# A transformer's second attention on one core: scores from halved operands in 32 rows, and normalisation on two engines

## The chip, the cores and the metric

The kernel runs on one core of a Trainium2 chip. A core has a matrix engine (TensorE, PE in the profile, with its weight loads shown as PEld), a vector engine (VectorE, DVE), an engine for activation functions (ScalarE, ACT), a general engine (GpSimd, POOL) and one that mainly issues transfers (SyncE, SP). Each works through its own queue of instructions in a fixed order; semaphores tie them together. Matrix products land in PSUM, everything else lives in SBUF, and DRAM is reached by DMA. The metric is the device time of one execution in microseconds (us), lower is better.

## The reference

The input x is 16 sequences of 256 tokens with 128 features, in float32. Four residual steps follow one another:

```
x = x + attention_a(layernorm(x))      # 2 heads of 64, rotary embedding on half of each head
x = x + ffn(layernorm(x))              # 128 -> 512 -> 512 -> 512 -> 128, ternary weights
x = x + attention_b(layernorm(x))      # 16 heads of 8, masked
x = x + ffn(layernorm(x))
```

The second attention is the one that the change touches:

```
mask = arange(n)[:, None] <= arange(n)[None, :]
scores = einsum('bhki,bhqi->bhkq', k, q) / sqrt(8)
scores = where(mask, scores, -10000)
probs = softmax(scores, axis=2)                 # over the third axis, inside 'bhkq'
combined = einsum('bhkq,bhkl->bhql', probs, v)
```

The softmax runs over the keys as scores are laid out here, and masked scores count as -10000 and not as minus infinity. The kernel therefore needs the maximum of each row of scores, and a correction for the masked ones.

## The kernel before

**Blocks.** The 4096 tokens are cut into 8 blocks of 512 (two sequences each). Each block goes through attention a, FFN f, attention b and FFN g. Blocks are independent, so the stages of several blocks overlap.

**The plan.** The kernel doesn't issue instructions as it goes. A class `Plan` (from line 95) records every operation with the engine, an assumed duration, and the tiles that it reads and writes. `laid` (line 166) then lays them out one after the other: among the operations that are ready it takes, for each engine, those that could start within 0.144 us of the earliest (a change of activation table or of PE's tiling mode weighted by `WEIGH`), and among these the one of the lowest rank by `ORDER` (line 337). Operations recorded with `either` (line 147) name two or three engines, and the layout takes the one that has room. `emit` (line 275) issues everything in that order; therefore nearly every instruction carries line 287 in the profile, and one tells groups by their tiles.

**Buffers.** SBUF tiles come from groups with a fixed number of slots: `w6`, `w4` and `w8` all appear as `w` in the profile, as do the four single PSUM banks. `s` is the one four-bank PSUM tile for scores of both attentions. `h` holds the FFN's hidden layers in two fp32r parts, a rounded one and the remainder, `u` an FFN layer before it is split, `hl` its last layer.

**Layernorm** (`layernorm_T`, line 651). Per block DVE computes mean and variance (`st`, `mv`), POOL the inverse root (`rstd`), DVE normalises in four instructions of 128x128 (`xh`), PE transposes, and an eviction writes `xT`. The attentions use `xhattn`, the FFNs `xhffn`.

**Attention b, inputs** (`attention_b_inputs`, line 802). PE makes q and k for all 16 heads, 8 features each, so that head 4g + a sits in rows 32g + 8(3 - a) and following. q is evicted twice (`qb`), scaled by `qscale`; k four times (`kb`), each time with all heads but one set to zero by `kmask`. A product over 32 rows with the masked k gives the scores of one head of a group g, and four groups g run in the four 32-row parts of the array.

**Attention b, maxima** (`attention_b_max`, line 833). For each sequence and each a of four, eight fp32 matmuls in 32 rows (per head one of 128 and one of 256 columns) write scores to `s`, four bf16 matmuls add a mask (`eye`, `hide`), and DVE takes the maxima of three 128-key blocks (`m3`). The negative maxima go into unused rows of a transposed tile (`nm`), and two DVE operations (`q2`) add them to q, so that one row of the next product subtracts them.

**Attention b, probabilities** (`attention_b`, line 892). For each a, eight fp32 matmuls in 32 rows write the transposed scores minus the maxima, ACT takes exp (1536 columns), POOL clears the masked half of the diagonal blocks (affine select), and PE multiplies with `vp` (v with a column of ones, in 32-column mode). The rest divides, transposes and projects.

**FFN** (`ffn`, line 1038). fp32r matmuls of 512 columns, two parts per operand, silu and gelu on ACT, products and splits on DVE, ACT or POOL. The ranks place FFN work as filling between the attentions' steps.

**The fork.** `product` (line 1001) has a general form for weights that fp32r can't hold exactly; a branch at run time picks it. With the given weights it isn't taken.

Of the kernel before, what the change touches and what calls it, by code (L numbers as in the profile page):

```python
# [94 lines left out]
class Plan:  # L95
# [4 lines left out]
    SWITCH = 0.15  # L100
    WEIGH = 0.78
# [45 lines left out]
    def either(self, *ways):  # L147

        (engine, us, name, a, k), *rest = ways
        r = self(engine, us)  # L150
        getattr(r, name)(*a, **k)
        for engine, us, name, a, k in rest:
            other = Op(engine, us, r.op.rank)
            other.calls.append((name, a, k))
            r.op.others.append(other)
# [10 lines left out]
    def laid(self):  # L166
# [28 lines left out]
        for _ in range(len(self.ops)):  # L195
            best = None
            for e, ops in ready.items():
# [23 lines left out]
                if not cands:  # L221
                    continue

                first = min(a + self.WEIGH * c for a, c, _ in cands)
                at, cost, op = min(
                    (x for x in cands if x[0] + self.WEIGH * x[1] <= first + 0.144),
# [63 lines left out]
class _Recorder:  # L290
# [19 lines left out]
P = 128  # L310
B, T, E = 16, 256, 128
TB = 4
# [25 lines left out]
    (INPUT, "a"): (47, 0.9),  # L338
    (MAIN, "a"): (52, 1.0),
    (NORM, "f"): (298, 0),  # L340
    (FILL, "f"): (118, 3.3),
    (INPUT, "b"): (76, 0.9),
    (MAXIMA, "b"): (-22, 0),
    (MAIN, "b"): (14, 17.0),
    (NORM, "g"): (81, 0),
    (FILL, "g"): (180, 9.1),
}
LATER_AT = -89
# [23 lines left out]
def hybrid_kernel(ctx: ExitStack, tc: tile.TileContext, x, rows, cols, wa, wb, w12, h1, h2, w3, out):  # L372
# [5 lines left out]

    p = Plan(nc)

    def group(tag, slots, in_turn=False):
        g = Group(slots, in_turn)
        g.tag = tag
        return g
# [8 lines left out]
    g_24, g_16, g_32 = group("w6", 4), group("w4", 3), group("w8", 3)  # L393
    q_qkv, q_pT, q_qkT, q_qb, q_pa, q_kb = Group(2), Group(3), Group(2), Group(2), Group(2), Group(2)
    g_rope, g_oT, g_small = group("rope", 6), group("oT", 2), group("small", 16)
    g_vb, g_q2, g_wv, g_o, g_oTb = (group(n, k) for n, k in (("vb", 2), ("q2", 2), ("wv", 2), ("o", 2), ("oTb", 1)))
# [166 lines left out]

    pi = fixed([P, 4], "pi", I32)
    p("POOL", 0.1).iota(pi[:], pattern=[[0, 4]], base=0, channel_multiplier=1)
    wanta = fixed([P, 4], "wanta", I32)
    p("POOL", 0.1).iota(wanta[:], pattern=[[1, 4]], base=0, channel_multiplier=0)
    wantr = fixed([P, 4], "wantr", I32)
    p("POOL", 0.1).iota(wantr[:], pattern=[[-3, 4]], base=31, channel_multiplier=0)
    ai = fixed([P, 4], "ai", I32)  # L570
    ri = fixed([P, 4], "ri", I32)
    kmask = fixed([P, 4], "kmask")
    mrow4 = fixed([P, 4], "mrow4")
    kbias = fixed([P, 4], "kbias")
    qscale = fixed([P, 2], "qscale")
    qbias = fixed([P, 2], "qbias")
    mrow = fixed([P, 2], "mrow")
    s8 = 1.0 / math.sqrt(DB)
    o = p("DVE", 1.25)
    o.tensor_scalar(ai[:], pi[:], 3, 3, ALU.arith_shift_right, ALU.bitwise_and)  # L580
    o.tensor_scalar(ri[:], pi[:], 31, None, ALU.bitwise_and)
    o.tensor_tensor(kmask[:], ai[:], wanta[:], ALU.is_equal)
    o.tensor_tensor(mrow4[:], ri[:], wantr[:], ALU.is_equal)
    o.scalar_tensor_tensor(kbias[:], kmask[:], cols_sb[:, C_BK : C_BK + 1], mrow4[:], ALU.mult, ALU.add)
    o.tensor_scalar(qscale[:, 0:1], kmask[:, 3:4], -s8, s8, ALU.mult, ALU.add)
    o.tensor_scalar(qscale[:, 1:2], kmask[:, 3:4], s8, None, ALU.mult)
    o.tensor_scalar(qbias[:], qscale[:], cols_sb[:, C_BQ : C_BQ + 1], None, ALU.mult)
    o.tensor_reduce(mrow[:, 0:1], mrow4[:, 0:3], AX.X, ALU.max)
    o.tensor_copy(mrow[:, 1:2], mrow4[:, 3:4])
# [61 lines left out]
    def layernorm_T(i, what, bias=None):  # L651
# [16 lines left out]
        xh = sb([P, TB, E], f"xh_{what}{i}", g["xh"])  # L668
        for t in range(TB):
            p("DVE", 0.26).tensor_scalar(  # L670
                xh[:, t, :], XR[i][:, t, :], mv[:, t, 0:1], rstd[:, t : t + 1], ALU.subtract, ALU.mult
            )
# [54 lines left out]
    def attention_a(i, qkv, qkT):  # L727

        sc = p.tile(psum, [P, SEQS, HA, 2, T], F32, f"sa{i}", g_scores)
        for s in range(SEQS):  # L730
            o = p("PE", 0.87, "2r")
# [70 lines left out]
    def attention_b_inputs(i):  # L802

        xT = layernorm_T(i, "b", ob[:])
        q = sb([P, 2, TOK], f"qb{i}", g_16, q_qb)
        pq = bank(f"pqb{i}", ahead)
        p("PE", 0.45, "1", claim=[q]).matmul(pq[:], lhsT=wb_sb[:, 0:128], rhs=xT[:], start=True, stop=True)
        for c in range(2):
            by, plus = qscale[:, c : c + 1], qbias[:, c : c + 1]
            p.either(  # L810
                ("DVE", 0.72, "tensor_scalar", (q[:, c, :], pq[:], by, plus, ALU.mult, ALU.add), {}),
                ("ACT", 0.67, "activation", (q[:, c, :], pq[:], AF.Identity), {"bias": plus, "scale": by}),
            )
        k = sb([P, 4, TOK], f"kb{i}", g_32, q_kb)
        pk = bank(f"pkb{i}", ahead)
        p("PE", 0.45, "1", claim=[k]).matmul(pk[:], lhsT=wb_sb[:, 128:256], rhs=xT[:], start=True, stop=True)
        for a in range(4):
            by, plus = kmask[:, a : a + 1], kbias[:, a : a + 1]
            p.either(
                ("ACT", 0.67, "activation", (k[:, a, :], pk[:], AF.Identity), {"bias": plus, "scale": by}),  # L820
                ("DVE", 0.72, "tensor_scalar", (k[:, a, :], pk[:], by, plus, ALU.mult, ALU.add), {}),
            )
# [8 lines left out]
        return q, k, v  # L831

    def attention_b_max(i, s, q, k, v):
# [10 lines left out]
        for a in range(4):  # L844
            c = a // 3
# [340 lines left out]
```

## Time and profile before

| what | value |
|---|---|
| three timed runs | 823.2 us median, 822.59 to 823.42 |
| profiled execution | 823.35 us, of which the span of its instructions is 821.6 |
| mean granted PE clock in the span | 0.983 of full speed |
| PE busy | 762.0 us (93%), 6212 records |
| DVE busy | 538.2 us (66%) |
| ACT busy | 538.0 us (65%), of which 160.4 us are 125 table loads of 1.283 us |
| POOL busy | 222.9 us (27%) |
| matmuls of transposed scores `s<-q,w` | 1024 records, mean 347 ns |
| matmuls of scores for the maxima `s<-w,w` | 1024 records, mean 348 ns |
| DVE's maxima `m<-s` | 64 of 1755 ns |
| ACT's exp of the second attention `w<-s` | 64 of 1452 ns |
| POOL's causal select | 64 of 1119 ns |
| normalisation on DVE | 64 of 454 ns (`xhattn`), 64 of 389 ns (`xhffn`) |

Busy time of an engine is the union of its records. Matmuls overlap in the pipeline, so a group's cost on PE is best read from its start to the next group's start. An fp32 matmul leaves two records. PE's clock is lower only in the first tens of us. DMA is busy at the start, while inputs load, and with the outputs towards the end.

### The profile page before, as it was taken

Reading aid. Unit: us, or ns where it says so; the run is one execution under the profiler, and the core shown is the slowest. Engines: PE = TensorE matmul, PEld = TensorE weight load, DVE = VectorE, ACT = ScalarE, POOL = GpSimd, SP = SyncE. Lnnn points to the kernel's source line nnn. Section 1 sums busy time; section 2 is a strip of 40 time slices with the busy share of each in tenths; the row PEclk is TensorE's granted clock in tenths of the full one; section 3 lists DMA queues with packets and bytes.
Section 4 is the critical chain, followed back from the end, with each engine's and each line's share of the span. In section 5 each row is a group of like instructions: output and inputs, shape, how many; then the busy total and the mean of one; then the engine's idle time right before and its main releaser. Section 6 shows DMA issues by size and latency. Waiting matters only on the chain.

```text
span 821.6 us, 15080 instructions
## 1 busy us (share of the span) xinstructions
PE 762.0 (93%) x6212; PEld 536.1 (65%) x6212; DVE 538.2 (66%) x1129; ACT 538.0 (65%) x744; POOL 222.9 (27%) x322
## 2 busy tenths in 40 slices
PE   4688999999999999999999998999999999999997
PEld 2355666667577676667675765776776577676775
DVE  7897866877778486637847775763773576262551
ACT  3455887745946746974687475549468546989743
POOL 7654444110411403320233033113113301323200
PEclk9689999999999999999999999999999999999999
DMA  9400000000000000000000000000000000000000
GB/s 286 130 2 1 1 2 0 2 1 1 2 1 1 1 2 1 1 2 1 1 2 2 1 1 2 2 14 2 14 1 14 2 1 14 1 14 1 14 15 18
DMA packets 12191, 11.69 MB, mean 14 GB/s; under 512 B 720, under 2 KB 9424, under 8 KB 12112
## 3 DMA queue, kind: packets, MB, share of 16 engines
q1 hardware_dynamic: 10624, 7.61, 3.0%
q0 software_dynamic: 1200, 2.62, 0.9%
q8 instruction: 51, 0.84, 0.4%
q10 hardware_dynamic: 288, 0.39, 0.3%
q14 instruction: 28, 0.23, 0.1%
HBM read 8.53 MB, written 2.10 MB: 13 GB/s over the span
## 4 chain that ended last, share of the span: by engine, by line
PE 60%; DVE 20%; ACT 14%; issue 2%; POOL 1%; DMA 1%; SPq 0%; POOLq 0%; DVEq 0%; ACTq 0%
PE w L287 45%; PE s L287 15%; ACT w L287 6%; ACT L287 5%; DVE w L287 4%; DVE h L287 2%; DVE small L287 2%; DVE xhattn L287 2%; ACT u L287 2%; DVE u L287 2%; DVE m L287 1%; DMA x<-in_x 1%; ACT h L287 1%; DVE o L287 1%; DVE xlffn L287 1%
## 5 line engine op out<-in xcount | busy, mean ns | idle before, releaser
L287 PE MATMUL w<-h,h_sb 128*128 128x512 f32 x1024 | 281.2, 412 | 3.7 <-DVE h L287 1.3
L287 PEld LDWEIGHTS w<-h,h_sb 128*128 128x128 f32 x1024 | 181.3, 189 | 56.0 <-issue 8.7
L287 ACT ACT_TABLE_LOAD x125 | 160.4, 1283 | 4.1 <-PEq L1177 1.3
L287 POOL TENSOR_SCALAR_AFFINE_SELECT w<-w 128x1024 f32<-128x1024 f32 x64 | 71.6, 1119 | 289.2 <-ACT w L287 282.9
L287 DVE TENSOR_REDUCE m<-s 128x12 f32<-128x1536 f32 x64 | 112.3, 1755 | 50.3 <-PE s L287 49.9
L287 ACT ACTIVATE u<-w,cols_sb 128x512 f32<-128x512 f32 x128 | 87.1, 687 | 76.5 <-PE w L287 75.9
L287 ACT ACTIVATE w<-s 128x1536 f32<-128x1536 f32 x64 | 92.9, 1452 | 32.1 <-PE s L287 30.7
L287 DVE TENSOR_TENSOR h<-u,h 128x512 fp32r<-128x512 f32 x105 | 74.9, 713 | 42.5 <-ACT h L287 39.8
L287 ACT ACTIVATE hl<-w,cols_sb 128x512 f32<-128x512 f32 x64 | 42.1, 687 | 53.7 <-PE w L287 53.4
L287 DVE SCALAR_TENSOR_TENSOR u<-w,cols_sb,u 128x512 f32<-128x512 f32 x64 | 47.7, 746 | 32.9 <-ACT u L287 26.6
L287 PE MATMUL s<-w,w 32*128 32x128 f32 (+1 forms) x1024 | 60.0, 348 | 3.9 <-DVE m L287 2.1
L287 PE MATMUL w<-w_sb,hl 128*128 128x128 f32 x512 | 63.1, 277 | 0.1
L287 PE MATMUL s<-q,w 32*128 32x256 f32 (+1 forms) x1024 | 59.8, 347 | 3.4 <-ACT w L287 2.7
L287 PEld LDWEIGHTS s<-q,w 32*128 32x128 f32 x1024 | 46.2, 184 | 25.5 <-ACT w L287 13.3
L287 PEld LDWEIGHTS w<-w_sb,hl 128*128 128x128 f32 x512 | 60.0, 192 | 2.8 <-ACT hl L287 1.9
L287 PE MATMUL w<-w,vp 128*32 128x256 f32 (+1 forms) x1024 | 55.3, 335 | 4.3 <-POOL w L287 2.8
L287 PE MATMUL w<-xTffn,w_sb 128*128 128x512 f32 x128 | 56.9, 445 | 2.2 <-DVE u L287 1.6
L287 DVE TENSOR_TENSOR x<-w,x 128x512 f32<-128x512 f32 (+1 forms) x40 | 23.2, 579 | 46.5 <-PE w L287 46.0
L287 PE MATMUL w<-xlffn,w_sb 128*128 128x512 f32 x128 | 52.5, 410 | 0.0
L287 PEld LDWEIGHTS s<-w,w 32*128 32x128 f32 x1024 | 34.3, 185 | 24.6 <-DVE m L287 8.9
L287 POOL TENSOR_TENSOR h<-u,h 128x512 fp32r<-128x512 f32 x23 | 29.6, 1290 | 65.3 <-ACT h L287 55.2
L287 PEld LDWEIGHTS w<-w,vp 128*32 128x32 f32 x1024 | 27.1, 110 | 29.5 <-issue 8.7
(153 smaller groups left out, 1068.2 us busy)
## 6 DMA issues: line engine op xcount, KB each, us to landing
w<-in_h SPq DMA_DIRECT2D x2, 1024.0 KB, 14.7
h_sb<-in_h POOLq DMA_DIRECT2D x2, 1024.0 KB, 11.6
out<-x SPq DMA_DIRECT2D x8, 256.0 KB, 2.3
x<-in_x SPq DMA_DIRECT2D x7, 256.0 KB, 8.0
w<-in_w SPq DMA_DIRECT2D x1, 512.0 KB, 8.8
w_sb<-in_w POOLq DMA_DIRECT2D x1, 512.0 KB, 7.2
rows_sb<-in_rows ACTq DMA_DIRECT2D x1, 384.0 KB, 7.1
x<-in_x SPq DMA_DIRECT2D x2, 128.0 KB, 3.2
```

The costliest lines, as they stand in the source:

```text
L287: getattr(getattr(self.nc, self.ENGINES[op.engine]), name)(*a, **k)
```

## The change

The second attention's q and k become two halves each: the value rounded to fp32r (high) and the remainder (low). Each half is written to DRAM twice by SP, by an access pattern that repeats it, and read back by POOL so that a head's 32 rows hold all pairings of high and low: 8 features x 2 x 2. Every head then has its own 32 rows, and one fp32r product over 32 rows gives the exact score. q is scaled by scaling its weights once at the start. The maxima are split into two halves as well and enter the transposed scores through extra matmuls with a selection matrix `pick`. The matmuls' columns change: two of 256 per head for the maxima, and four of 256 per head for the transposed scores (two of k, two of `pick`). The layernorms' normalisation may go to ACT, as scale and shift; POOL makes the shift. The planner's assumed costs, the ranks and the slots of some groups change, and with them the whole order.

```diff
-    SWITCH = 0.15
-    WEIGH = 0.78
+    SWITCH = 0.17
+    WEIGH = {"ACT": 0.81, "PE": 0.07}
...
-                first = min(a + self.WEIGH * c for a, c, _ in cands)
+                weigh = self.WEIGH.get(e, 0.0)
+                first = min(a + weigh * c for a, c, _ in cands)
                 at, cost, op = min(
-                    (x for x in cands if x[0] + self.WEIGH * x[1] <= first + 0.144),
+                    (x for x in cands if x[0] + weigh * x[1] <= first + 0.077),
...
 ORDER = {
-    (INPUT, "a"): (47, 0.9),
-    (MAIN, "a"): (52, 1.0),
...
+    (INPUT, "a"): (-446, 27.2),
+    (MAIN, "a"): (-466, 77.1),
...
-    g_24, g_16, g_32 = group("w6", 4), group("w4", 3), group("w8", 3)
+    g_24, g_16, g_32 = group("w6", 4), group("w4", 3), group("w8", 4)
...
+    pick4 = fixed([P, 4], "pick4")
+    pick = fixed([P, 4, P], "pick", F32R)
...
+    p("DVE", 0.46).tensor_copy(pick[:], pick4[:].unsqueeze(2).to_broadcast([P, 4, P]))
...
+    p("POOL", 0.3).tensor_scalar(wb_sb[:, 0:P], wb_sb[:, 0:P], s8, None, ALU.mult)
...
+        shift = small([P, TB], f"sh_{what}{i}")
+        p("POOL", 0.45).tensor_tensor(shift, mv[:, :, 0], rstd[:], ALU.mult)
+        p("POOL", 0.3).tensor_scalar(shift, shift, -1.0, None, ALU.mult)
         for t in range(TB):
-            p("DVE", 0.26).tensor_scalar(
-                xh[:, t, :], XR[i][:, t, :], mv[:, t, 0:1], rstd[:, t : t + 1], ALU.subtract, ALU.mult
+            by, mean = rstd[:, t : t + 1], mv[:, t, 0:1]
+            p.either(
+                ("DVE", 0.26, "tensor_scalar", (xh[:, t, :], XR[i][:, t, :], mean, by, ALU.subtract, ALU.mult), {}),
+                ("ACT", 0.24, "activation", (xh[:, t, :], XR[i][:, t, :], AF.Identity), {"bias": shift[:, t : t + 1], "scale": by}),
             )
...
-        for c in range(2):
-            by, plus = qscale[:, c : c + 1], qbias[:, c : c + 1]
...
-        for a in range(4):
-            by, plus = kmask[:, a : a + 1], kbias[:, a : a + 1]
...
+        for name, c0, bias in (("q", 0, C_BQ), ("k", P, C_BK)):
...
+            hl = sb([P, 2, TOK], f"{name}hl{i}", g_16, q_hl, F32R)
+            p("PE", 0.45, "1", claim=[hl]).matmul(pp[:], lhsT=wb_sb[:, c0 : c0 + P], rhs=xT[:], start=True, stop=True)
             p.either(
+                ("ACT", 0.67, "activation", (hl[:, 0, :], pp[:], AF.Identity), {"bias": plus}),
+                ("DVE", 0.72, "tensor_scalar", (hl[:, 0, :], pp[:], plus, None, ALU.add), {}),
+            )
+            p("DVE", 0.77).scalar_tensor_tensor(hl[:, 1, :], pp[:], plus, hl[:, 0, :], ALU.add, ALU.subtract)
+
+            shape = [P, 2, 2, TOK]
+            far = p.fixed(dram.tile(shape, F32, name=f"far_{name}{i}"), shape)
+            for part in range(2):
+                p("SP", 0.55, lag=2.4).dma_start(
+                    out=far[:, part] if name == "q" else far[:, :, part],
+                    in_=hl[:, part, :].bitcast(F32).unsqueeze(1).to_broadcast([P, 2, TOK]),
+                )
+            t4 = sb([P, 4, TOK], f"{name}4{i}", g_32, None, F32R)
+            p("POOL", 0.85, lag=6.0).dma_start(out=t4[:], in_=far.rearrange("(g r) x y k -> (r x y) g k", g=4))
...
-            o = p("PE", 1.2, ("4r", "1"))
-            for qt, c0, w in ((0, 0, P), (1, P, T)):
-                for g in range(4):
+            o = p("PE", 0.28 + 0.15 + 0.42, ("4r", "1"))
+            for qt, c0 in ((1, 0), (0, T)):
+                for a in range(4):
+                    rows = slice(32 * a, 32 * a + 32)
                     o.matmul(
-                        lhsT=q[gs, c, t0 + qt * P : t0 + (qt + 1) * P],
-                        rhs=k[gs, a, t0 : t0 + w],
+                        sc[:, a, c0 : c0 + T],
+                        lhsT=q[rows, g, t0 + qt * P : t0 + (qt + 1) * P],
+                        rhs=k[rows, g, t0 : t0 + T],
...
+        o.tensor_copy(both[:, :, :, 0:8:2].bitcast(F32R), m32)
+        o.tensor_tensor(both[:, :, :, 1:8:2].bitcast(F32R), m32, both[:, :, :, 0:8:2], ALU.subtract)
...
-        for c in range(2):
-            p("DVE", 0.39).scalar_tensor_tensor(
-                q2[:, c, :], pm[:, 0:T], mrow[:, c : c + 1], q[:, c, t0 : t0 + T], ALU.mult, ALU.add
-            )
+        evict(mT[:], pm[:, 0:T], T)
...
-                o = p("PE", 0.66, "4r", claim=[pT])
-                for kt, bs, w in ((0, slice(0, 3, 2), T), (1, slice(1, 2), P)):
-                    for g in range(4):
+                o = p("PE", 0.54, "4r", claim=[pT])
+                for kt, c0 in ((1, 0), (0, T)):
+                    for add in range(2):
+                        for a in range(4):
+                            rows = slice(32 * a, 32 * a + 32)
+                            o.matmul(
+                                st[:, a, c0 : c0 + T],
+                                lhsT=pick[rows, g, :] if add else k[rows, g, t0 + kt * P : t0 + (kt + 1) * P],
+                                rhs=mT[rows, :] if add else q[rows, g, t0 : t0 + T],
...
-    nc = bacc.Bacc("TRN2", target_bir_lowering=False, num_devices=1, dynamic_dma_scratch_size=8192)
+    nc = bacc.Bacc("TRN2", target_bir_lowering=False, num_devices=1, dynamic_dma_scratch_size=4096)
```

Left out are the setup of the masks that fall away, the general form's smaller buffers, and the order in which `cols`, `attn_w` and `attn_b` rows are laid on the host (head 4a + g stands in rows 32g + 8a on the way to its own 32 rows).

## The prediction

> **What bounds the kernel now.** I read the shares of busy time first, then the slices, the chain that ended last, one table of windows, and then single groups in the timeline.
>
> From the page: busy time by engine, the TensorE (PE) slices with the clock, and the chain.
>
> ```profile
> PE 762.0 (93%) x6212; PEld 536.1 (65%) x6212; DVE 538.2 (66%) x1129; ACT 538.0 (65%) x744; POOL 222.9 (27%) x322
> ...
> PE   4688999999999999999999998999999999999997
> ...
> PEclk9689999999999999999999999999999999999999
> ...
> PE 60%; DVE 20%; ACT 14%; issue 2%; POOL 1%; DMA 1%; SPq 0%; POOLq 0%; DVEq 0%; ACTq 0%
> PE w L287 45%; PE s L287 15%; ACT w L287 6%; ACT L287 5%; DVE w L287 4%; DVE h L287 2%; DVE small L287 2%; DVE xhattn L287 2%; ACT u L287 2%; DVE u L287 2%; DVE m L287 1%; DMA x<-in_x 1%; ACT h L287 1%; DVE o L287 1%; DVE xlffn L287 1%
> ```
>
> The windows (span, then busy us and instructions of each engine, granted clock, DMA) split the span into the start, the first attention, the second attention's stage and the tail.
>
> ```profile
> 0.00:82.00 82.00, 58.05 (x269) 34.97 (x270) 67.88 (x218) 39.32 (x95) 50.97 (x103) 0.85 0.34 105
> ...
> 164.00:766.00 602.00, 578.25 (x5219) 409.21 (x5218) 381.08 (x703) 404.92 (x461) 135.86 (x154) 1.00 0.01 3
> 766.00:822.00 56.00, 48.01 (x254) 37.88 (x252) 26.60 (x50) 26.75 (x37) 3.63 (x4) 0.99 0.06 17
> ```
>
> PE is busy 96% of the second attention's 602 us (578.25), VectorE (DVE) 63% and ScalarE (ACT) 67%: that stage is PE's, and PE time taken out of it should shorten it. The second attention's scores (tile s) hold 15% of the chain, 126 us. In the timeline, PE alone around one group of scores for the maxima:
>
> ```profile
> 227.75 0.94 PE L287 MATMUL s<-w,w 32*128 32x128 f32 x16
> 228.62 0.61 PE L287 MATMUL s<-hide,eye 128*128 128x256 bf16 x4
> 229.06 0.60 PE L287 MATMUL w<-ident,oT 128*128 128x128 f32 x4
> 229.42 2.58 PE L287 MATMUL w<-h,h_sb 128*128 128x512 f32 x10
> 231.93 0.39 PE L287 MATMUL s<-w,w 32*128 32x128 f32 x3
> ```
>
> and around one transposed group:
>
> ```profile
> 564.68 0.94 PE L287 MATMUL s<-q,w 32*128 32x256 f32 x16
> 565.55 0.74 PE L287 MATMUL w<-h,h_sb 128*128 128x512 f32 x2
> ```
>
> From start to next start a maxima group holds PE 0.87 us, the four mask matmuls (bf16, 256 columns) 0.44, a transposed group 0.87. Four heads run side by side: 16 records of 0.27 to 0.43 us end within 0.94.
>
> **The sum's base.** The profiled execution took 823.35 us (span 821.6 and 1.75 around it), the median of the three timed runs 823.2: the same within 0.02%. I count from 823.35.
>
> **PE: what the halves save.** A mask matmul passes 256 columns in 0.11 us (0.44 / 4). Both old groups stream 256 + 128 columns per head in fp32; at four passes that is 1.5 x 0.11 x 4 = 0.66, so 0.87 - 0.66 = 0.21 goes into entering and leaving the 32-row mode. The new maxima group has 2 matmuls of 256 columns per head and the new transposed group 4 (two of keys, two that add the maxima through `pick`). fp32r passes 512 columns in 0.233 us: the ten at 229.42 take 2.51 to the next start, the four at 234.96 take 1.11, and 1.40 / 6 = 0.233. Twice the mask's 0.11 is 0.22, so an fp32r weight load costs 0.013 more, and a 256-column step 0.123. New groups: 0.21 + 2 x 0.123 = 0.46 and 0.21 + 4 x 0.123 = 0.70. Saved: 64 x (0.87 - 0.46) + 64 x (0.87 - 0.70) = 26 + 11 = 37 us. The best end is a step of 0.11: 64 x (0.44 + 0.22) = 42. No row has fp32r in 32 rows, so the other end is a step in which load (0.189 by the fp32r load row) and stream (0.11) follow each other, 0.30: the groups become 0.81 and 1.41 and PE loses 31. I take 37: the 32-row fp32 rows already hide four loads per head in 0.66 us of streaming, and the mask row hides one load per 0.11. Nothing else on PE changes: masks, projections and P.V keep their counts, and changes of tiling mode, counted in the two planned orders, are 408 before and 407 after.
>
> The Trainium skill, "TensorE: Matmul & The Clock Gate", Part 3, The mechanism, speaks against this: a weight load overlaps a running matmul only when its row group differs. Taken strictly, every step on the same 32 rows would pay load plus stream, 0.30 by the rows above, and the sum would end at 858. The trace's 32-row fp32 groups contradict the strict reading: four loads of 0.185 per head and 0.66 of streaming would be 1.4 us, and the group took 0.87.
>
> **DVE and ACT.** DVE loses 25 of the scaled q and k evictions (0.81 us: 20), 32 adds of the maxima into q (0.478 by `q<-w,mrow,w`: 15), 79 normalisations (44 x 0.454 + 35 x 0.389: 34) and 8 low halves of h that go to POOL (6): 75. It gains 16 low halves of q and k (0.746 by the u row: 12), 12 high halves (0.69 to 0.81: 9), 32 small ops on the maxima (0.19 to 0.24: 7) and evictions that the new order puts there (9 mT and 8 more oTb of 0.42, 9 w of 0.68, 7 probabilities of 0.44: 16): 44. Net -31. ACT loses 17 table loads (125 to 108 in the planned order, 1.283 each: 22), 23 q and k evictions (17) and evictions worth 12; it gains 79 normalisations. No row has ACT on 128x128 from SBUF: 0.32 by its 128x32 row, 0.51 by its 128x256 row; 0.40 lies between, 32; with high halves and copies of 8, net -11. Both engines are covered by PE and get lighter, so I book 0 for them; where PE waits less for them, that is rival 2's gain.
>
> **POOL.** It gains 64 ops of 128x4 (0.24: 15), 8 low halves (1.29: 10) and 16 DMA issues (0.78: 12), 37 on 223; it stays near a third of the span, and books 0 in time. But its queue now also waits. Each read of q4 and k4 waits on POOL for the halves to land in DRAM, and behind it in POOL's order stand the causal selects (for block 1 directly behind), for which P.V on PE waits. SP carries nothing but these writes between the input loads and the outputs, so nothing is held behind them there. Where ACT normalises it waits for the shift, POOL's two new ops, 0.48 after the scale; before, PE stood for the normalised rows in three places (9.0 us in all), so the end is 3 x 0.48 = 1.4, and I book 0. The halved DMA scratch has no row: at best nothing, at worst POOL's second read of a pair is issued only when the first has landed (4.3 us by the next paragraph's quiet rows), eight times, 34 us of POOL time with half of it before selects; I book 0, since POOL issued 1 MB twice in a row before (1.55 us together), and leave the 17 to rival 4's size.
>
> **The trip through DRAM.** Per block four 512 KB writes on SP and two 1 MB reads on POOL. Rows: `out<-x` 256 KB lands in 2.3 us on quiet queues; `h_sb<-in_h` 1 MB in 11.6 and `w<-in_w` 512 KB in 8.8 in the crowded start, where windows of 3 us show up to 405 GB/s. At 400 GB/s 256 KB are 0.65, so the fixed part is about 1.65; a quiet 512 KB write is 2.95, and a pair of reads ends 5.2 + 1.65 = 6.9 after the first issue. Block 0: after k's projection the chain is 0.69 (high) + 0.75 (low) + 0.5 (SP) + 2.95 + 0.8 (POOL) + 6.9 = 12.6. PE's planned order has 9.5 us of work there, by the rows above. So PE stands about 3 us, or 15 with the crowded rows. Later blocks write long before; their reads wait until the block two earlier has left its tiles (four slots hold two blocks). From there to the first group that needs them PE has 8.4 us (block 2), 9.6 (block 6) and 11 to 16 (the others); the pair needs 0.8 + 6.9 = 7.7. Quiet: nothing late, I take 1 in all. Crowded, 13 each: 15 in all. Booked: +4, ends 0 and 30.
>
> **Sum:** 823.35 - 37 + 4 = 790.
>
> **Rivals.**
> 1. *The sum as above*, 790, own range 780 to 800: 0.58.
> 2. *More*: steps of 0.11 (-42), no DRAM wait, and the chain's DVE part (20%, 164 us) shrinks with DVE's load (31 of 538, 6%: -9). 823 - 42 - 9 = 772. For it: DVE and ACT both get lighter. Against: PE's waits in the second attention's stage are only 4% in busy time. 0.09.
> 3. *Half is lost*: PE reaches the next wait earlier and stands there, for DVE's maxima (1.755 us each on the one score buffer) or ACT's exp with its table load. For it: DVE and ACT hold 34% of the chain. Against: the order is laid anew and FFN matmuls fill the gaps. 823 - 18 + 4 = 809. 0.13.
> 4. *DRAM late with crowded durations*: 823 - 37 + 30 = 816. Against: outside the start DMA shows 0.01 of its share. 0.04.
> 5. *The other side*: the 32-row fp32r steps don't hide their own weight loads. The place is the 64 + 64 groups; six steps and two mode changes equal the old 1.74 us at a step of 0.22, above which PE loses: (1.74 - 0.42) / 6. At 0.30 it is 823 + 31 + 4 = 858. For it: twice as many loads per streamed time as in any row here. Against: the load rows above. 0.16, of which 0.02 falls near a step of 0.22, no change.
>
> **How the numbers follow.** About 0.2%, 1.6 us, can be told from no change. Faster: 0.58 + 0.09 + 0.13 + 0.04 = 0.84; within 0.2%: 0.02; slower: 0.14. The range goes from rival 2 (772) to rival 4 (816); outside it lie rival 5 (0.16) and a little of rival 2.
>
> **What would show it.** Right: score groups of 0.46 and 0.70 from start to next start, four side by side; PE busy near 725; 108 table loads; no PE wait over 2 us on a DMA but before the first second-attention scores; q4 and k4 landing 4 to 7 us after issue. Wrong: 32-row matmul records one after another instead of in fours, or steps above 0.2; POOL's selects standing behind a DMA; PE idle ahead of s growing by what the groups lost; landings above 10 us outside the start.

## The result, and the profile after

The change makes the kernel slower: 847.81 us (median of 4 runs, 843.80 to 853.38) against 822.89 us before (4 runs on the same chip), a ratio of 1.0316 with a 95% interval of 1.0251 to 1.038. The prediction was 790 us, faster. The profiled execution took 853.38 us, the longest of the four, 0.7% above the median; its span is 851.6. The four differ with the mean clock that PE was granted: 0.991 in the shortest, 0.980 in the longest.

The page of the changed kernel: busy time by engine, the TensorE (PE) slices, its clock, and the chain that ended last.

```profile
PE 797.9 (94%) x6724; PEld 572.1 (67%) x6724; DVE 509.8 (60%) x1068; ACT 526.9 (62%) x773; POOL 261.3 (31%) x411
...
PE   4788899989999989999999999999999999999996
...
PEclk9899999998999989999999999999999999999999
...
PE 73%; DVE 11%; ACT 9%; POOL 3%; issue 2%; DMA 1%; DVEq 0%; ACTq 0%; POOLq 0%
PE w L291 51%; PE s L291 23%; ACT w L291 4%; ACT L291 2%; DVE small L291 2%; DVE w L291 2%; DVE u L291 1%; DVE h L291 1%; DVE m L291 1%; ACT u L291 1%; DMA w<-far_k 1%; POOL rstdattn L291 0%; POOL w L291 0%; POOL rope L291 0%; ACT h L291 0%
```

VectorE (DVE) and ScalarE (ACT) got lighter, as meant. PE did not: its busy time rose from 762.0 to 797.9 us, and the scores (tile s) went from 15% of the chain to 23%. Span less PE busy time was 821.6 - 762.0 = 59.6 before and is 851.6 - 797.9 = 53.7 now. So the 30.0 us between the two profiled spans (24.9 between the medians) are +35.9 of PE busy and -5.9 of PE standing. A little of the 35.9 is clock: 0.980 granted here against 0.983 before, and 762.0 x 0.983 / 0.980 is 764.3. The other 33.6 are what has to be explained.

The windows (start and end, length, then busy us of PE, PEld, DVE, ACT and POOL with their instructions, granted clock, DMA share, GB/s) show that this holds in the second attention's stage, where PE is busy 98% of the time (584.48 of 597):

```profile
0.00:82.00 82.00, 57.81 (x301) 35.34 (x302) 65.89 (x206) 48.92 (x130) 59.06 (x131) 0.94 0.33 105
...
188.00:785.00 597.00, 584.48 (x5561) 419.85 (x5562) 343.39 (x631) 373.12 (x448) 161.20 (x202) 0.99 0.16 55
785.00:852.00 67.00, 57.41 (x313) 46.49 (x311) 27.24 (x50) 33.49 (x48) 2.88 (x5) 0.97 0.05 14
```

The timeline of PE, around one group of scores for the maxima and one transposed group (start, duration, instructions in a row of one kind):

```profile
425.81 1.15 PE L291 MATMUL s<-w,w 32*128 32x256 f32 x16
426.89 0.61 PE L291 MATMUL s<-hide,eye 128*128 128x256 bf16 x4
427.25 2.58 PE L291 MATMUL w<-h,h_sb 128*128 128x512 f32 x10
...
434.11 0.71 PE L291 MATMUL s<-w,w 32*128 32x256 f32 x8
434.46 0.48 PE L291 MATMUL s<-mT,pick 32*128 32x256 f32 x4
434.76 0.61 PE L291 MATMUL s<-w,w 32*128 32x256 f32 x8
435.00 0.49 PE L291 MATMUL s<-mT,pick 32*128 32x256 f32 x4
435.42 1.16 PE L291 MATMUL w<-w_sb,hl 128*128 128x128 f32 x8
```

From start to next start a maxima group holds PE 426.89 - 425.81 = 1.08 us, where the old one held 0.87 and the forecast said 0.46; a transposed group holds 435.42 - 434.11 = 1.31, where the old one held 0.87 and the forecast said 0.70. These two stand for the rest: the medians over the groups of each kind are 1.08 and 1.31. The reason stands in the counts. The maxima's group has eight matmuls in the code, two for each of four heads, and 16 records here; the products with `pick` have as many records as matmuls (4 + 4). Two records for a matmul is how fp32 looked in the profile before. The page's groups say the same for the whole run:

```profile
L291 PE MATMUL s<-w,w 32*128 32x256 f32 x2048 | 156.2, 404 | 6.8 <-ACT w L291 4.3
...
L291 PE MATMUL s<-mT,pick 32*128 32x256 f32 x512 | 62.5, 468 | 0.0
```

`s<-w,w` are the products of q4 and k4: 512 for the maxima and 512 for the transposed scores, but 2048 records. `pick` has 512 matmuls and 512 records. So q4 and k4 were multiplied as full 32-bit floats (fp32), and only `pick` as fp32r, the rounded 32-bit type whose products leave one record each.

**Why.** The new q4 and k4 are declared fp32r. But a slot of SBUF gets its type from whichever tile is made in it first, and a later tile is given another view only if it is neither of the two 32-bit types (`Plan.tile`, the same in both kernels):

```
def make(slot):
    if slot not in group.homes:
        kind = F32R if dtype == F32R else F32
        group.homes[slot] = pool.tile([shape[0], group.words], kind, ...)
    home = group.homes[slot][:, 0:words]
    if dtype not in (F32, F32R):
        home = home.bitcast(dtype)
```

q4 and k4 live in group `w8`, together with the exact copies of the weights and attention a's probabilities, which are fp32 and come first. All four slots become fp32, and q4 and k4 are read as fp32 in all 8 blocks. The halves themselves (group `w4`, first used by `qkT`) go the same way: the profile after has `w<-w,cols_sb` writing f32 where the control below has fp32r. So the high half is not rounded, and by the code the low half then holds next to nothing; no view shows its values. An fp32 product needs no halves: the kernel before had none.

### The profile page after: what moved, and what is told of

The parts are those of the page before. It is cut to its first block, busy times and chain, and to the rows that moved or that the text cites. A ratio compares the mean times of both kernels' runs of the same rounds, so it can differ in the third digit from the quotient of the medians.

```text
span 851.6 us, 16291 instructions
## 1 busy us (share of the span) xinstructions
PE 797.9 (94%) x6724; PEld 572.1 (67%) x6724; DVE 509.8 (60%) x1068; ACT 526.9 (62%) x773; POOL 261.3 (31%) x411
## 4 chain that ended last, share of the span: by engine, by line
PE 73%; DVE 11%; ACT 9%; POOL 3%; issue 2%; DMA 1%; DVEq 0%; ACTq 0%; POOLq 0%
PE w L291 51%; PE s L291 23%; ACT w L291 4%; ACT L291 2%; DVE small L291 2%; DVE w L291 2%; DVE u L291 1%; DVE h L291 1%; DVE m L291 1%; ACT u L291 1%; DMA w<-far_k 1%; POOL rstdattn L291 0%; POOL w L291 0%; POOL rope L291 0%; ACT h L291 0%
## 5 line engine op out<-in xcount | busy, mean ns | idle before, releaser
L291 PE MATMUL w<-h,h_sb 128*128 128x512 f32 x1024 | 273.3, 408 | 3.1 <-DVE h L291 2.1
L291 PEld LDWEIGHTS w<-h,h_sb 128*128 128x128 f32 x1024 | 184.3, 190 | 51.4 <-issue 5.7
L291 PE MATMUL s<-w,w 32*128 32x256 f32 x2048 | 156.2, 404 | 6.8 <-ACT w L291 4.3
L291 PEld LDWEIGHTS s<-w,w 32*128 32x128 f32 x2048 | 87.9, 186 | 51.0 <-issue 17.6
L291 ACT ACTIVATE w<-s 128x1536 f32<-128x1536 f32 x64 | 92.8, 1449 | 44.5 <-PE s L291 43.3
L291 DVE TENSOR_TENSOR h<-u,h 128x512 fp32r<-128x512 f32 x97 | 68.3, 704 | 40.7 <-ACT h L291 38.3
L291 POOL TENSOR_TENSOR h<-u,h 128x512 fp32r<-128x512 f32 x31 | 39.5, 1281 | 118.2 <-ACT h L291 118.2
L291 PE MATMUL w<-xTffn,w_sb 128*128 128x512 f32 x128 | 58.7, 459 | 7.1 <-DVE u L291 3.2
L291 PE MATMUL s<-mT,pick 32*128 32x256 f32 x512 | 62.5, 468 | 0.0
L291 ACT CAST h<-u 128x512 fp32r<-128x512 f32 x65 | 40.3, 619 | 2.8 <-DVE u L291 0.8
```

Source lines behind the costliest of these rows:

```text
L291: getattr(getattr(self.nc, self.ENGINES[op.engine]), name)(*a, **k)
```

## The experiments

All ratios are to the kernel before on the same chip, with 95% intervals. The runs come from several chips, on which the kernel before took 821.18 to 822.89 us, so differences of 2 us between two runs can't be told from none. "PE stands" means span less PE busy time. Theory P is the above: the loss is the price of q4's and k4's products in fp32.

### A control, and the products in one pass

A view of `w8` as fp32r alone would leave tiles in it that are written as fp32. The control makes its slots fp32r and has everything that lives there written as fp32r: attention a's probabilities are written as fp32r, the exact copies of h1 and h2 and their run-time test go, and only w12 is tested; the kernels built on it below share this. The high halves are rounded here. It still reads q4 and k4 as fp32 (two of the four casts are shown).

```diff
-                kind = F32R if dtype == F32R else F32
+                kind = F32R if dtype == F32R or group.tag == "w8" else F32
...
-            if dtype not in (F32, F32R):
+            if dtype != group.kinds[slot]:
...
-            pp = sb([P, 2, HA, 2, T], f"pa{i}_{s}", g_32, q_pa)
+            pp = sb([P, 2, HA, 2, T], f"pa{i}_{s}", g_32, q_pa, F32R)
...
+                        lhsT=q[rows, g, t0 + qt * P : t0 + (qt + 1) * P].bitcast(F32),
+                        rhs=k[rows, g, t0 : t0 + T].bitcast(F32),
```

> The changed kernel with three edits that the next run needs: the buffers of q4 and k4 are declared as fp32r (attention a's probabilities, which share them, are therefore rounded to fp32r), the high halves are really rounded, and the run-time test of the weights looks at w1 and w2 alone (h1 and h2 are left out: 2 MB less to load and two ACT passes of 1.9 us less at the start). Both score products still read q4 and k4 as fp32, as in the changed kernel's trace (two records for each matmul). Theory P (the halves' products run as fp32 in four passes, and that is what costs): 838 to 848, score groups 1.08 us (maxima) and 1.31 us (transposed) from start to next start. Theory R (fp32r in 32 rows would not stream faster anyway): the same, 838 to 848. Theory O (the new order, the DRAM trip and the normalisation cost the time): the same. Below 830 the edits themselves would matter, and the next runs are to be read against this one only.

Measured: 846.77 us (846.39 to 850.26), ratio 1.0294 [1.0276, 1.0312], PE busy 795.9: the changed kernel's time within its spread (847.81). It stands for the change in what follows.

The second kernel is the control without the four `.bitcast(F32)`: both products read fp32r, in the same planned order.

> As the control, but both products read q4 and k4 as fp32r; the planned order is the same. Theory P: one record for each matmul, groups 0.46 and 0.70 us, PE saves 64 x (1.08 - 0.46) + 64 x (1.31 - 0.70) = 79 us, and since PE is busy 94% of the span at least half shows: 765 to 805, below the kernel before (823). Theory R: groups at 0.8 and above, within 2% of the control, 825 to 860. Theory O: the groups shrink, but the time stays above 823.

Measured: 782.91 us (780.83 to 783.83), ratio 0.9515 [0.9491, 0.9539]. The page:

```profile
PE 718.7 (92%) x5700; PEld 510.5 (65%) x5700; DVE 505.7 (65%) x1056; ACT 529.0 (68%) x782; POOL 259.2 (33%) x410
...
PE 59%; DVE 16%; ACT 13%; DMA 5%; issue 4%; POOL 2%; SPq 0%; DVEq 0%; ACTq 0%; POOLq 0%
PE w L292 47%; PE s L292 12%; ACT w L292 5%; ACT L292 4%; DMA w<-far_k 4%; DVE small L292 3%; DVE w L292 3%; ACT u L292 2%; DVE m L292 2%; DVE u L292 2%; DVE h L292 2%; POOL w L292 1%; DMA x<-in_x 1%; DVE x L292 1%; DMA far_k<-w 1%
...
L292 PE MATMUL s<-w,w 32*128 32x256 f32 x1024 | 73.4, 331 | 9.3 <-ACT w L292 4.7
```

and its timeline:

```profile
427.39 0.51 PE L292 MATMUL s<-w,w 32*128 32x256 f32 x8
427.83 0.61 PE L292 MATMUL s<-hide,eye 128*128 128x256 bf16 x4
...
454.90 0.39 PE L292 MATMUL s<-w,w 32*128 32x256 f32 x4
455.13 0.29 PE L292 MATMUL s<-mT,pick 32*128 32x256 f32 x4
455.25 0.29 PE L292 MATMUL s<-w,w 32*128 32x256 f32 x4
455.36 0.29 PE L292 MATMUL s<-mT,pick 32*128 32x256 f32 x4
455.58 1.16 PE L292 MATMUL w<-w_sb,hl 128*128 128x128 f32 x8
```

1024 records for 1024 matmuls, and groups of 427.83 - 427.39 = 0.44 and 455.58 - 454.90 = 0.68 us: the forecast's 0.46 and 0.70. The medians over the groups of each kind are the same. PE busy time falls by 77.2 us against the control, at the same granted clock of 0.984; 63.9 us arrive in the time, and PE stands longer (62.2 us against 52.6). In one and the same order, the type as which q4 and k4 are read decides between 3% slower and 5% faster: that is the cause.

### Each product alone

The same control, with one pair of the four casts removed. Shown is the maxima's pair; the second run removes the other.

```diff
-                        lhsT=q[rows, g, t0 + qt * P : t0 + (qt + 1) * P].bitcast(F32),
-                        rhs=k[rows, g, t0 : t0 + T].bitcast(F32),
+                        lhsT=q[rows, g, t0 + qt * P : t0 + (qt + 1) * P],
+                        rhs=k[rows, g, t0 : t0 + T],
```

> The control a_control (846.77 us) with one difference: the scores for the maxima read q4 and k4 as fp32r, the transposed scores still as fp32; same planned order. Theory P (each kind of product costs on PE what its group shows from start to next start): the maxima's group falls from 1.08 us to the 0.44 that b_onepass showed, 64 x 0.64 = 41 us less PE work. Of the 79 us that both kinds together took from PE's work, 64 came out as time, 0.8 of it, so 846.8 - 33 = 814 (806 to 820). Rival Q (the maxima feed DVE's reduction of 1.757 us on the one score buffer, so a faster group only makes PE wait there, and the whole gain lies in the transposed scores): 838 to 848.

> The control a_control (846.77 us) with one difference: the transposed scores read q4 and k4 as fp32r, the scores for the maxima still as fp32; same planned order. Theory P: the group falls from 1.31 us to the 0.68 that b_onepass showed, 64 x 0.63 = 40 us less PE work, 0.8 of it in time: 815 (807 to 820), and the gains of this run and of c_max_onepass add up to b_onepass's 64. Rival Q (the whole gain lies here): 783 to 795.

Measured: the maxima alone 810.78 us, 0.9863 [0.9833, 0.9893]; the transposed scores alone 820.42 us, 0.9983 [0.9968, 0.9998]. Against the control that is -36.0 and -26.4, together 62.4 of the 63.9 of both: the prices add up. Rival Q (all of the gain on one side) falls. The maxima came in the expected range; the transposed scores a little short of theirs. PE busy time, first of the maxima's kernel, then of the other's:

```profile
PE 755.8 (93%) x6212; PEld 543.3 (67%) x6212; DVE 506.5 (63%) x1056; ACT 530.0 (66%) x782; POOL 259.8 (32%) x410
```

```profile
PE 760.4 (93%) x6212; PEld 538.7 (66%) x6212; DVE 505.6 (62%) x1056; ACT 529.2 (64%) x782; POOL 259.1 (32%) x410
```

In both PE's work falls by the groups' price (40.1 and 35.5 us against 795.9). With the maxima alone span less busy is 53.4, as in the control (52.6); with the transposed scores alone it is 61.3. So it is behind the faster transposed groups that PE stands more; what for was not traced.

### The trip through DRAM

In the one-pass kernel the chain names reads of the halves, some of them long:

```profile
178.47 4.17 DMA far_k<-w
183.18 7.11 DMA w<-far_k
...
233.87 10.78 DMA w<-far_k
...
359.89 13.44 DMA w<-far_k
```

while PE's waits (us in total, times, longest) give them little:

```profile
PE s L292 <- DMA w<-far_k: 2.9, 3, 1.4
```

To see which of the two views holds the price, POOL reads 1 MB of an input in place of the halves, so that no read waits for a write. The writes still run, the reads have their old size, and the scores are of other numbers.

```diff
+                if op.instead is not None:
+                    k['in_'] = op.instead
...
-            p("POOL", 0.85, lag=6.0).dma_start(out=t4[:], in_=far.rearrange("(g r) x y k -> (r x y) g k", g=4))
+            o = p("POOL", 0.85, lag=6.0)
+            o.dma_start(out=t4[:], in_=far.rearrange("(g r) x y k -> (r x y) g k", g=4))
+            o.op.instead = h1.rearrange("(g p) k -> p g k", g=4)
```

> b_onepass (782.91 us) in the same planned order, with POOL reading 1 MB of the input h1 by the same pattern (rows of 2 KB) where it read the halves back. The four writes of each block still go to DRAM, but no read waits for them; the scores are then of other numbers, and the output is not the reference's. Theory T (the trip costs what PE stood for its reads, 2.9 us in three waits, as the prediction booked 4): 778 to 783. Rival U (the trip holds up more than PE's waits show, since its reads are 4% of the chain, 31 us): 750 to 770.

Measured: 780.74 us (779.58 to 781.28), 0.9497 [0.9467, 0.9527], 2.2 us below the one-pass kernel by the medians, with ranges that overlap. One read is left in the chain, and PE's waits for reads go from 2.9 us to 1.1:

```profile
357.80 12.66 DMA w<-in_h
...
PE s L295 <- DMA w<-in_h: 1.1, 2, 0.6
```

The trip's pieces in the chain went from 35.5 us (the four above) to 12.7, and the time by 2.2 at most. So the chain's share names the DMA and does not price it; PE's waits were the better guide. What the reads themselves cost, which this run keeps, was not tested.

### The engine that normalises

The one-pass kernel in the same order, with the 82 normalisations that the plan had given to ACT issued by DVE at the same place.

```diff
+                if op.stays:
+                    op.emitted = op.engine, op.calls
                 op.engine, op.us, op.calls = way.engine, way.us, way.calls
...
-            for name, a, k in op.calls:
+            engine, calls = op.emitted or (op.engine, op.calls)
+            for name, a, k in calls:
...
-            )
+            ).stays = True
```

> b_onepass (782.91 us) in the same planned order, with the 82 normalisations that the plan had put on ACT issued by DVE at the same place. DVE gains about 82 x 0.27 = 22 us of work, ACT loses 82 x 0.41 = 34. Theory O (both engines are covered by PE, the normalisation's engine is worth nothing by itself): 778 to 789. Rival N (DVE, 16% of the chain, is the engine that is short, and ACT's part in the normalisation is a gain): 795 to 806.

Measured: 804.14 us (802.78 to 805.68), 21.2 us slower than the one-pass kernel and inside Rival N's range. The page:

```profile
PE 725.8 (91%) x5700; PEld 515.3 (64%) x5700; DVE 531.2 (66%) x1138; ACT 498.2 (62%) x700; POOL 259.9 (32%) x410
```

DVE gains 25.5 us and ACT loses 30.8, neither is near full, and yet the time moves by nearly what DVE gained. PE stands 75.2 us where it stood 62.2. Its busy time also grows by 7.1 us, with the same matmuls, and that fits the clock: it was granted 0.975 here against 0.984, and 718.7 x 0.984 and 725.8 x 0.975 are 707 and 708. Why the clock is lower was not tested. So in this order, "covered by PE" was no ground for a price of nothing. Whether an order laid for DVE from the start would lose as much, this run can't say.

### Normalisation alone, in the kernel before

Before, with the normalisation on either engine and POOL's shift, everything else (scores, ranks, slots, costs) as it was.

```diff
+        shift = small([P, TB], f"sh_{what}{i}")
+        p("POOL", 0.45).tensor_tensor(shift, mv[:, :, 0], rstd[:], ALU.mult)
+        p("POOL", 0.3).tensor_scalar(shift, shift, -1.0, None, ALU.mult)
...
-            p("DVE", 0.26).tensor_scalar(
+            p.either(
```

> The kernel before with only the other half of the change: normalisation on DVE or ACT, with POOL's shift; the old scores, ranks and planner constants. Theory P: it lightens DVE and costs PE nothing, so 810 to 826. Theory O: slower than 828.

Measured: 839.29 us (834.53 to 841.04), 1.0188 [1.0148, 1.0228]: slower, as Theory O had it. PE stands 71.2 us where it stood 59.6. Then the same plan with those 90 normalisations issued by DVE at their places:

> f_before_norm (839.29 us: before, with normalisation by either engine and POOL's shift) in the same planned order, with the 90 normalisations that the plan had put on ACT issued by DVE at the same place, as before does everywhere. Theory O (what f_before_norm lost against before, 17 us, comes of the order laid anew, not of the engine): 834 to 844. Rival N (ACT's normalisations, 90 x 0.41 = 37 us more on ACT, are the loss): 820 to 828.

Measured: 848.7 us (847.3 to 852.25), 1.0336 [1.0294, 1.0378]. Both of its expectations miss. Issuing ACT's part on DVE did not win the 17 us back but cost 9.4 us more, so Rival N falls for this order, which was laid with ACT's help. The likely rest is the order, which `either` lays anew, together with POOL's 32 shifts of two operations each. These two were not told apart.

### What an order is worth

Two runs hold nearly all the work and move the order. First the changed kernel, planned with the products' costs in fp32:

```diff
-            o = p("PE", 0.28 + 0.15 + 0.42, ("4r", "1"))
+            o = p("PE", 0.86 + 0.15 + 0.42, ("4r", "1"))
...
-                o = p("PE", 0.54, "4r", claim=[pT])
+                o = p("PE", 1.14, "4r", claim=[pT])
```

> The changed kernel with the planner's PE costs of the two score steps set to what the trace shows, less the mode change (0.28 to 0.86 and 0.54 to 1.14); nothing else changes but the order that follows from them. Theory P (PE's own work binds): 840 to 856, within 1% of the changed kernel. Rival M (the order was laid for groups that are 0.6 us shorter than they are, and the waits from that are the loss): 10 us faster or more, below 838.

Measured: 868.3 us (866.45 to 868.52), 1.0551 [1.0529, 1.0573], 20.5 us above the changed kernel and outside both expectations. Here, telling the planner nearer to the truth about the products made the order worse. ACT has 131 table loads here, and 108 in the changed kernel:

```profile
PE 803.4 (93%) x6724; PEld 572.2 (66%) x6724; DVE 509.8 (59%) x1072; ACT 558.9 (65%) x802; POOL 251.6 (29%) x401
...
L291 ACT ACT_TABLE_LOAD x131 | 168.1, 1283 | 14.1 <-DVE small L291 8.0
```

Second, the whole computation in one pass, without the control's omissions: q4 and k4 as fp32r tiles of one sequence in a group of their own, so that the fp32 tiles can stay in `w8`.

```diff
-    g_24, g_16, g_32 = group("w6", 4), group("w4", 3), group("w8", 4)
+    g_24, g_16, g_32 = group("w6", 4), group("w4", 3), group("w8", 2)
+    g_t4 = group("t4", 4)
...
+        for s in range(SEQS):
+            for name, far in tiles:
+                t4 = sb([P, 4, T], f"{name}4{i}_{s}", g_t4, None, F32R)
```

> The whole computation with one pass: after, with q4 and k4 as fp32r tiles of one sequence each (four slots of 128x1024) in a group of their own, read from DRAM in four reads of 512 KB per block instead of two of 1 MB, the high halves written as fp32r, the weights' exact copies and attention a's probabilities in the two remaining slots of w8; the order is laid anew. Theory P: PE does the work of b_onepass, and the order laid anew is worth up to 1.5% either way by the runs so far: 771 to 795. Rival V (four slots hold only two sequences, so that each read waits for the sequence before to leave its tiles, and PE stands for the landing of a quiet pair, some 4 us, at most of the 16 sequences): 800 to 845.

Measured: 818.68 us (816.99 to 820.59), 0.9972 [0.9957, 0.9987]: barely faster than before. The page, and PE's longest waits:

```profile
PE 728.0 (89%) x5700; PEld 511.2 (63%) x5700; DVE 517.0 (63%) x1083; ACT 541.7 (66%) x783; POOL 260.5 (32%) x415
```

```profile
PE w L292 <- ACT u L292: 12.8, 20, 1.7
PE s L292 <- DVE m L292: 10.9, 19, 1.2
PE w L292 <- ACT xhattn L292: 10.3, 2, 8.6
...
PE s L292 <- DMA t<-far_k: 2.6, 1, 2.6
```

The time lies where rival V put it, but not for V's reason: PE stands once for a read, 2.6 us, and for the rest mostly behind ACT and DVE. The score groups are as short as in the one-pass kernel (medians 0.44 and 0.67); of the 34.5 us between the two spans, 9.3 are PE's busy time and 25.2 are PE standing (87.4 against 62.2). Fewer slots and another order came together here and weren't told apart.

### Versions that beat both

The one-pass kernel with the run-time test of all weights restored, h1 and h2 in pieces of 128x1024 through two slots of `w6`. What remains otherwise than in the changed kernel is that attention a's probabilities are rounded to fp32r. With the ranks of the change the plan got longer by its own reckoning (762 against 741), so two pairs of ranks were altered:

```diff
-    (INPUT, "a"): (-446, 27.2),
+    (INPUT, "a"): (-413.0, 25.5),
...
-    (NORM, "f"): (410, 65.2),
+    (NORM, "f"): (434.0, 52.2),
...
+                exact.append(p.tile(work, [P, 2, DH], F32, f"w{len(exact)}", g_24, q_exact))
```

> The whole run-time test of the weights again (h1 and h2 in pieces of 128x1024 through two slots of w6, w12 in w4), the rest as b_onepass: q4 and k4 read as fp32r, attention a's probabilities kept as fp32r (rounded, the one thing that this kernel computes otherwise). The plan keeps after's assumed costs; two pairs of ranks (inputs of attention a, norms of FFN f) are changed so that the plan ends at 743 of its own us, where b_onepass's ends at 741 and the same kernel with after's ranks at 762. Theory O (what the order is worth shows in the plan's own end, with some 42 us on top as in b_onepass): 778 to 792. Rival R (the plan's end says nothing of the chip at this size, since its costs are not the chip's): anywhere from 795 to 820, as g_sequence_tiles fell.

Measured: 789.05 us (785.22 to 790.39), 0.9586 [0.9548, 0.9624]: faster than both kernels of this study. Then the same kernel planned with the costs that the runs had shown. Against the changed kernel it alters one pair of ranks, another one; the two pairs above are back at the changed kernel's:

```diff
-    (MAIN, "b"): (119, 2.6),
+    (MAIN, "b"): (142.0, 2.9),
...
-                ("ACT", 0.24, "activation", (xh[:, t, :], XR[i][:, t, :], AF.Identity), {"bias": shift[:, t : t + 1], "scale": by}),
+                ("ACT", 0.41, "activation", (xh[:, t, :], XR[i][:, t, :], AF.Identity), {"bias": shift[:, t : t + 1], "scale": by}),
...
-            o = p("PE", 0.28 + 0.15 + 0.42, ("4r", "1"))
+            o = p("PE", 0.81, ("4r", "1"))
...
-                o = p("PE", 0.54, "4r", claim=[pT])
+                o = p("PE", 0.68, "4r", claim=[pT])
```

> The same kernel, planned with the costs that the runs showed (maxima 0.81, transposed scores 0.68, ACT's normalisation 0.41 instead of 0.85, 0.54 and 0.24), and one pair of ranks changed; the plan ends at 758 of its own us. Theory O (true costs make the plan's end nearer to the chip's, so it comes out with some 25 to 40 on top): 783 to 798, and above or at most level with k_whole_old_costs. Rival W (wrong costs are what made the orders of after and f_before_norm poor, and true ones give the better order whatever its planned end): 765 to 778.

Measured: 805.12 us (802.83 to 806.9), 0.9789 [0.9754, 0.9823]. Rival W falls; Theory O's range is missed too, by 7 us, though its order of the two kernels holds. The two pages:

```profile
PE 722.1 (92%) x5700; PEld 514.8 (65%) x5700; DVE 516.0 (65%) x1086; ACT 520.3 (66%) x760; POOL 258.6 (33%) x409
```

```profile
PE 729.6 (91%) x5700; PEld 517.9 (64%) x5700; DVE 514.9 (64%) x1080; ACT 521.8 (65%) x763; POOL 265.8 (33%) x413
```

The same matmuls in two orders are 16 us apart: 8.9 in PE's standing and 7.5 in its busy time. Of these 7.5 about 5 fit the granted clock (0.976 and 0.969; 722.1 x 0.976 / 0.969 = 727.3). The plan's own end (743 and 758) ranked them rightly and was 46 and 47 us short of both.

## Why the prediction was wrong, by its own steps

**The base** held: 823.35 against 822.89 measured again.

**PE, -37: this is the step that failed.** It said "The new maxima group has 2 matmuls of 256 columns per head and the new transposed group 4", priced at "a 256-column step 0.123" in fp32r. The number of matmuls was right, and so was the fp32r step: with fp32r the groups took 0.44 and 0.68, that is a step of (0.44 - 0.21) / 2 = 0.115 and a transposed group of 0.21 + 4 x 0.115 = 0.67; the 0.24 between the two groups are two steps and give 0.12 without the estimate of 0.21. What failed is the assumption under the price, that the products of q4 and k4 run in fp32r at all. In the changed kernel they take (1.08 - 0.21) / 2 = 0.435 a step, and the transposed group 0.21 + 2 x 0.435 + 2 x 0.115 = 1.31, just what was measured. The term should have been 64 x (1.08 - 0.87) + 64 x (1.31 - 0.87) = 13 + 28 = +42; PE's busy time rose by 35.9. A drop of about the size of the gap shows in the FFN's `w<-h,h_sb`, which kept PE busy 281.2 us before and 273.3 after; why was not traced. The Trainium skill, "FP8 and Floating Point Precision", TensorE Precision Notes, gives a true fp32 product four passes. The two steps measured here, 0.435 against 0.115, are a ratio of 3.8, close to it.

**The rivals** lacked this one: that the change doesn't do what it says. The forecast took the declared type of a tile for the type that the matmul reads. The lines that decide it are in the code before, unchanged and so not in the diff. The fifth rival (slower, 858) came nearest in time, by a mechanism that the runs refute: steps of 0.115 with four loads of 0.184 running beside them. Its sign, steps above 0.2, did come, but only in the products of q4 and k4: the two steps of `pick` add 1.31 - 1.08 = 0.23, 0.115 each, as forecast. In the one-pass kernel all steps are near 0.115 with load records of 0.184. With that falls the strict reading of the Trainium skill, "TensorE: Matmul & The Clock Gate", Part 3, The mechanism, by which loads on the rows in use would wait for the matmul.

**DVE and ACT.** The sizes were right: DVE -28.4 (forecast -31), ACT -11.1 (forecast -11), and 108 table loads. Whether their price of nothing was right is open: the two engines got lighter and PE stood 5.9 us less, but in the one-pass order giving the normalisations back to DVE costs 21 us. An ACT normalisation was put at 0.40; the records show 0.48, and three in a row take 1.25.

**POOL, 0:** 261.3 us busy against 260 forecast, and PE waits for its selects 5.0 us in all, where it waited 6.0 before.

**The trip, +4:** no larger than booked, as far as PE's waits show it, by other numbers. Its DMAs (KB each, median us from issue to landing):

```profile
far_q<-w SPq DMA_DIRECT2D x16, 512.0 KB, 3.8
far_k<-w SPq DMA_DIRECT2D x16, 512.0 KB, 4.1
w<-far_q POOLq DMA_DIRECT2D x8, 1024.0 KB, 6.2
w<-far_k POOLq DMA_DIRECT2D x8, 1024.0 KB, 8.6
```

The writes land in 3.8 and 4.1 instead of 2.95, and single reads took up to 13.4 us in the one-pass kernel, but PE has work meanwhile: before the first scores, where 3 us were booked, it stands 0.85 us in the changed kernel, and 2.9 us in all in the one-pass kernel. Taking the reads' wait for the writes away is worth 2.2 us at most.

**The sum** comes out for the one-pass kernel, which does what the change says: 782.91 against 790, with PE busy 43.3 us less than before (37 booked) and standing 2.6 us more (4 booked for the trip). That it lands so near is in part luck with the order. The sum has no term for the new order, and three other kernels with the same fp32r products took 789.05, 805.12 and 818.68 us, the last outside the range of 772 to 816.

## What to carry to other kernels

When a change's gain rests on an operand's type, follow that type to the memory that the instruction reads: slots shared by several tiles, views, and who uses a slot first are often outside the diff. After a run, count records per matmul before anything else: two for one told here in a single line of the page what 36 us of PE time were. And where a planner lays out the order, put its own spread, 16 to 20 us here for nearly the same work, into the range of any change that makes it plan again. And don't book a moved operation at nothing because the engine is half busy: in one order here 25.5 us more on DVE cost 21.2.

## What the runs showed that was not expected

- The chain that ended last gave 4% (31 us) to DMA reads; without their wait for the writes the chain's share fell by more than half and the time by 2.2 us at most.
- 25.5 us more on a DVE that is busy 65% cost 21.2 us, in an unchanged order.
- Six kernels with the same matmuls and fp32r products, from 780.74 to 818.68 us, have PE busy times of 717.4 to 729.6 us. Busy time times granted clock is 705 to 708 in five of them, and 715 in the one with tiles of a sequence. So a good part of what PE's busy time grows by in a worse order goes with a lower granted clock.
- Costs nearer to the chip's came with worse orders twice: 868.3 against 847.81, and 805.12 against 789.05 (there with other ranks too).
- Four fp32r matmuls of 256 columns, side by side in 32 rows each, step every 0.115 us with their own loads of 0.184 hidden.
